# The gate of a hybrid network's second layer, moved into the fill of the feed-forward layer behind it

## Chip, cores, metric

The kernel runs on one core of one Trainium2 chip. A core has five engines, each with an instruction queue of its own that it works through in order: TensorE (PE in the profile; its weight loads are PEld), VectorE (DVE), ScalarE (ACT), GpSimd (POOL) and SyncE (SP), which issues most transfers. Engines wait for each other by semaphores. The metric is the time of one execution in microseconds; lower is better.

## The reference, cut to what matters

Four layers work on an image of 4 x 128 channels x 64 x 64. Only the end of the second and the beginning of the third take part in the change:

```python
# layer 1, its end: o is the state-space branch, turned back to channels
o = (o - mu) * lax.rsqrt(var + 1e-05) * bn_g + bn_b            # over batch and image
g = jax.nn.sigmoid(einsum('bihw,io->bohw', o, conv4_w) + conv4_b)
x = g * x + x
# layer 2: tokens of 128 channels
t = _to_tokens(x)                                              # a transpose
y = _ln_t(t)
attn = products of cos(y + theta) within groups of 8
x1 = layernorm(y + attn)
q = cos(phi) * cos(x1[..., :8])
ffn = relu(q @ w1.T + b1) @ w2.T + b2                          # 8 -> 2048 -> 128
t = t + layernorm(x1 + ffn)
```

The mean and variance of o run over all images, so no gate can be taken before the last map of o is there.

## The kernel before

The whole image stays in on-chip memory as X, 128 partitions x 16384 columns. In the second layer (`layer1`) X holds channels on the partitions; in the third (`layer2`) it holds tokens, 128 x 128 blocks turned in place. All arithmetic is float32.

**End of `layer1`.** The branch's 32 maps of 128 x 512 are stored to device memory as they are made (`kept`, the profile's `o<-o`), with their statistics in `bst` (psy is their psum tile). Behind the last one the statistics are joined (`mv`, line 1404), the normalisation is folded into the weights and bias of the 1x1 convolution (`conv4_w`, `sb`, lines 1404 to 1415), and then 32 gates and 32 turnings are written out, each turning two steps behind its gate:

- `gate(k)`: load map k (`oin`, four buffers, SP's queue, line 1421), a matmul of two passes into `psg`, a sigmoid on ScalarE into `g`, and (g + 1) * X on VectorE back into X;
- `to_tokens(k)`: four 128 x 128 transposes into one psum bank `psf`, and a copy back into X, by VectorE for odd k and by ScalarE for even k.

All but the loads go through `InOrder` (line 82 is its helper, which is why most rows of the profile have line 82): their order on each engine is the order of the program. The loads and what is not wrapped are placed by a scheduler.

**`layer2`.** First its weights: w1T (four loads of 16 KB behind a memset by GpSimd), w2T (1 MB), two zeroed buffers, and the cosine of phi (`cphi`, lines 1503 to 1508). Then 16 groups of 8 token blocks run through a software pipeline. A position p has eight slots; in position p, group p goes through the two big matmuls (`hidden` into `phh`, `rectify` into `hid`, `summed` into `pff`), while group p + 3 gets its first norm (steps a: `moments`, `variance`, `root`, `a_norm`, `a_turns`, `a_less`), group p + 2 its cosines, products and second norm (steps b), and group p - 1 its last norm (steps d). The positions run from -3 to 16. The first three, -3 to -1, have no or hardly any big matmuls: they fill the pipeline. In them the order is: statistics of a (VectorE), root (ScalarE), norm into u (VectorE), u + theta into c (GpSimd), reduction of the angle k, a (VectorE), absolute value and sine (ScalarE), products and u + a (GpSimd), statistics and norm of b (VectorE), gain and bias on x1 (GpSimd), then the angles of q, its sine and its spread into `q8`, which is transposed (`pqt`), copied (`qT`) and fed to `hidden`. The psum pool `ph` has four banks, all under the tag `phh`.

ScalarE evaluates its functions from table sets: the root, the sine and the sigmoid lie in different sets, and a change between them is an instruction of its own, ACT_TABLE_LOAD.

Of the kernel before, what the change touches and what calls it, by code (L numbers as in the profile page):

```python
# [8 lines left out]
F32 = mybir.dt.float32  # L9
I32 = mybir.dt.int32  # L10
AF = mybir.ActivationFunctionType
ALU = mybir.AluOpType
AX = mybir.AxisListType
PSUM = bass.MemoryType.PSUM
DRAM = bass.MemoryType.DRAM

P = 128
NB = 4
# [70 lines left out]
class Kernel:  # L89
# [815 lines left out]

    def layer1(self):

# [4 lines left out]
        tc, X = self.tc, self.X  # L914
        plain = self.nc
        nc = plain
        NG = 8
        GS = NT // NG
        with ExitStack() as ctx:
            cp = ctx.enter_context(tc.tile_pool(name="l1c", bufs=1))  # L920
            sp = ctx.enter_context(tc.tile_pool(name="l1s", bufs=2))
            gp = ctx.enter_context(tc.tile_pool(name="l1g", bufs=2))
            kp = ctx.enter_context(tc.tile_pool(name="l1k", bufs=2))
            dram = ctx.enter_context(tc.tile_pool(name="l1d", bufs=1, space=DRAM))
            pm = ctx.enter_context(tc.tile_pool(name="l1pm", bufs=4, space=PSUM))
            pp = ctx.enter_context(tc.tile_pool(name="l1pp", bufs=1, space=PSUM))

            def mm(name):
                return pm.tile([P, 512], F32, name=name, tag="mm")

            lin1_w = self.load(cp, "lin1_w", [P, P])
            fc_in4 = self.load(cp, "fc_in4", [P, P])
            conv4_w = self.load(cp, "conv4_w", [P, P])


            wx = self.load(cp, "in_w4", [P, 2, 257])
# [8 lines left out]
            ps = mm("psw2")  # L945
# [24 lines left out]

            Y = cp.tile([P, NT + 2 * GS, 2, DI], F32, name="Y")


            CY = [pp.tile([P, 2, 512], F32, name=f"CY{k}") for k in range(2)]
            kept = [dram.tile([P, 512], F32, name=f"o{k}") for k in range(NB * NG)]
            dw = self.col("dw_w")
            sh = [P, GS, 2]

# [83 lines left out]
            def s4(g, dr, j, w=P):  # L1062

                n, i = divmod(g, NG)
                r = GS * i + j
                c = r * P if dr == 0 else (NT - 1 - r) * P + 3
# [333 lines left out]
            nc = plain  # L1400
# [2 lines left out]
            mv = sp.tile([P, 2], F32, name="mv")  # L1403
            nc.vector.bn_aggr(mv, bst)
            sc = sp.tile([P, 1], F32, name="sc")
            sb = sp.tile([P, 1], F32, name="sb")
            nc.scalar.activation(sc, mv[:, 1:2], AF.Sqrt, bias=self.eps5)
            nc.vector.reciprocal(sc, sc)
            nc.vector.tensor_mul(sc, sc, self.col("bn_g"))
# [2 lines left out]
            ps = mm("psg")  # L1412
            nc.tensor.matmul(ps[:, 0:1], conv4_w, sb, start=True, stop=True)
            nc.vector.tensor_add(sb, ps[:, 0:1], self.col("conv4_b"))
            nc.vector.tensor_scalar(conv4_w, conv4_w, sc, None, ALU.mult)
            nc = InOrder(tc)

            def gate(k):
                ks = slice(k * 512, (k + 1) * 512)
                o = gp.tile([P, 512], F32, name="oin", tag="tm", bufs=4)  # L1420
                plain.sync.dma_start(o, kept[k])
                ps = mm("psg")
                nc.tensor.matmul(ps, conv4_w, o, start=True, stop=True)
                g = gp.tile([P, 512], F32, name="g", tag="yT")
                nc.scalar.activation(g, ps, AF.Sigmoid, bias=sb)
                nc.vector.scalar_tensor_tensor(X[:, ks], g, 1.0, X[:, ks], ALU.add, ALU.mult)

            def to_tokens(k):
                ps = mm("psf")
                for v in range(4):  # L1430
                    c = k * 512 + v * P
                    nc.tensor.transpose(ps[:, v * P:(v + 1) * P], X[:, c:c + P], self.ident)
                dst = X[:, k * 512:(k + 1) * 512]
                if k % 2:
                    nc.vector.tensor_copy(dst, ps)
                else:
                    nc.scalar.copy(dst, ps)

            for k in range(NB * NG + 2):
                if k < NB * NG:  # L1440
                    gate(k)
                if k >= 2:
                    to_tokens(k - 2)

    def flip(self):

# [65 lines left out]
    def layer2(self):  # L1512
# [4 lines left out]
        tc = self.tc  # L1517
        nc = self.nc
        GT, NG = 8, NB * NT // 8
        T = self.X.rearrange("p (t c) -> p t c", c=P)  # L1520
        with ExitStack() as ctx:
            cp = ctx.enter_context(tc.tile_pool(name="l2c", bufs=1))
# [4 lines left out]
            ph = ctx.enter_context(tc.tile_pool(name="l2ph", bufs=4, space=PSUM))  # L1527
# [16 lines left out]
            cphi = cp.tile([P, 8], F32, name="cphi")  # L1544
            self.cos(cp, cphi, self.row("phi"), [P, 8], "cphi")

            nc = InOrder(tc)
            V, S, G = nc.vector, nc.scalar, nc.gpsimd

            def bcast(name):  # L1550
# [1 line left out]

            def stream(g):
                return T[:, g * GT:(g + 1) * GT, :]

            st = {}

# [136 lines left out]
            def hidden(g, h, m):  # L1694
                phs = []
                for k in range(NK):
                    ks = slice(32 * k, 32 * k + 32)
                    phh = ph.tile([P, 512], F32, name="phh")
                    nc.tensor.matmul(phh, w1T[ks, m, :], st["qT", g, h][ks, :], start=True, stop=True)
                    phs.append(phh)  # L1700
                return phs

            def rectify(g, h, m, phs, on_vector):
                hids = []
                for k in range(NK):
                    f = NK * m + k
                    hid = hp.tile([P, 512], F32, name="hid")
                    if k in on_vector:
                        V.tensor_scalar(hid, phs[k], b1[:, f:f + 1], 0.0, ALU.add, ALU.max)
                    else:  # L1710
                        S.activation(hid, phs[k], AF.Relu, bias=b1[:, f:f + 1])
                    hids.append(hid)
                st["hid", g, h, m] = hids
# [9 lines left out]
            def on(g, step, *args):  # L1723
                if 0 <= g < NG:
                    step(*([g] + list(args)))

            ON_VECTOR = ((0, 1, 3), (1,), (1,), (1, 3), (1,), (1,), (1, 3), (1,))

            def slot(p, s):
                h, m = divmod(s, 4)  # L1730
                p1, h1, m1 = (p, *divmod(s + 1, 4)) if s < 7 else (p + 1, 0, 0)
                phs = hidden(p1, h1, m1) if 0 <= p1 < NG else None

                if s in (0, 4):
# [12 lines left out]
                if s == 0:  # L1747
                    on(a, lambda g: moments("A", g, stream(g), 0, GT))
                    on(b, lambda g: cosine(st["a", g]))
                    on(b, a_products)  # L1750
                elif s == 1:
                    on(d, d_add, 1)
                    on(a, lambda g: variance("A", g))
                    on(p + 1, lambda g: cosine(st["q", g]))
                    on(p + 1, b_spread)
                elif s == 2:
                    on(d, lambda g: moments("D", g, st["x1", g], 4, GT))
                    on(d, lambda g: variance("D", g))
                    on(b, lambda g: moments("B", g, st["u", g], 0, 4))
                elif s == 3:  # L1760
                    on(b, lambda g: moments("B", g, st["u", g], 4, GT))
                    on(b, lambda g: variance("B", g))
                    for name, g in (("D", d), ("A", a), ("B", b)):
                        on(g, lambda g: root(name, g))
                elif s == 4:
                    on(d, d_ready)
                    on(a, a_norm)
                elif s == 5:
                    on(p, d_add, 0)
                    on(b, b_norm)  # L1770
                    on(d, d_norm, 0)
                elif s == 6:
                    on(d, d_norm, 1)
                    on(d, d_sum)
                    on(a, a_turns)
                    on(p, lambda g: moments("D", g, st["x1", g], 0, 4))
                else:
                    on(a, a_less)
                    on(b, b_turns)

            for p in range(-3, NG + 1):
                for s in range(8):
                    slot(p, s)

# [621 lines left out]
@with_exitstack  # L2406
def tile_conv_attn_hybrid(ctx: ExitStack, tc: tile.TileContext, ins: dict, out: bass.AP):
    k = Kernel(ctx, tc, ins, out)
    k.layer0()
    k.layer1()  # L2410
    k.layer2()
    k.attention_maps(ctx)
    k.moe(2)
    k.attention()
    k.moe(3)
    k.flip()
# [79 lines left out]
```

## Time and profile before

| what | us |
|---|---|
| three runs, median (lowest to highest) | 5611.95 (5593.98 to 5615.91) |
| the profiled execution | 5601.23 |
| its span, first to last instruction | 5599.5 |
| layer 0, to about | 1225 |
| `layer1` up to its joined statistics, to about | 1957 |
| first gate matmul / last token copy | 1957.5 / 2006.2 |
| first statistics of `layer2` | 2004.9 |
| first `phh` matmul / first `pff` matmul | 2057.8 / 2070.0 |
| last `pff` matmuls of `layer2` | 2712 |
| all of the span: busy PE, DVE, ACT, POOL | 4991.9, 4016.3, 3113.9, 3073.1 |

Times inside the execution are counted from the span's start. A row of the profile is a group of instructions: line, engine, operation, tile written <- tiles read, shape. The windows view gives for a stretch how long each engine was busy in it, in microseconds with the number of instructions in brackets, and then the clock that TensorE was granted as a share of full speed, the mean busy share of the sixteen transfer engines, and GB/s. A busy TensorE at half clock does half the work, so both numbers are read together. A VectorE instruction's duration includes time in which it had begun and was held.

### The profile page before, as it was taken

The page shows a single profiled execution, that of the slowest core. Times are in us where ns is not written, and L with a number is a line of the kernel's source. Part 1 is how long each engine was busy: PE and PEld are TensorE (multiplying, and loading weights), DVE is VectorE, ACT ScalarE, POOL GpSimd, SP SyncE. Part 2 cuts the span into 40 slices and gives each one's busy share as a digit, 9 for nine tenths or more (in the row PEclk, how much of TensorE's full clock was granted, in tenths as well). Part 3 has the DMA queues.
Part 4 walks back from the last instruction along what each step waited for, and adds up shares of the span by engine and source line. Part 5 has one row for each costly group of instructions (what it writes and reads, how often), then busy time and mean ns, then how long its engine had stood idle before and what let it go on. Part 6 is the DMA issues. An engine that isn't in the chain of part 4 may idle for free. (4 is left out here: it accounts for less than half of the span.)

```text
span 5599.5 us, 62830 instructions
## 1 busy us (share of the span) xinstructions
PE 4991.9 (89%) x21718; PEld 2404.9 (43%) x21718; DVE 4016.3 (72%) x7854; ACT 3113.9 (56%) x3785; POOL 3073.1 (55%) x3027
## 2 busy tenths in 40 slices
PE   6898989879999859999887899989998998999887
PEld 3454444335656523333443344434433444344443
DVE  6888988758876578786698565666566666665796
ACT  1122222146655345555431689878978987889431
POOL 0525253314444324454399577666766776667597
PEclk8999999989988779999899899999999999999899
DMA  5545454400000020000000000000000000000001
GB/s 171 126 131 128 124 132 127 98 6 1 16 16 12 27 61 1 1 1 1 6 31 16 16 1 1 1 1 1 1 1 1 1 1 1 1 1 1 5 1 61
DMA packets 66743, 185.21 MB, mean 33 GB/s; under 512 B 13158, under 2 KB 16038, under 8 KB 64744
## 3 DMA queue, kind: packets, MB, share of 16 engines
q1 hardware_dynamic: 55792, 163.68, 9.9%
q0 software_dynamic: 6272, 12.86, 1.4%
q10 hardware_dynamic: 4344, 4.50, 0.3%
q8 instruction: 175, 2.87, 0.2%
q14 instruction: 160, 1.31, 0.1%
HBM read 131.63 MB, written 49.36 MB: 32 GB/s over the span
## 5 line engine op out<-in xcount | busy, mean ns | idle before, releaser
L82 POOL TENSOR_TENSOR r<-r 128x512 f32<-128x512 f32 (+1 forms) x1088 | 1349.0, 1241 | 661.9 <-DVE r L82 597.0
L82 DVE TENSOR_TENSOR r<-r,num 128x1024 f32<-128x1024 f32 (+1 forms) x1088 | 970.4, 927 | 564.3 <-PE num L82 514.1
L82 PE MATMUL D<-F,G 32*128 32x512 f32 (+3 forms) x4608 | 1218.8, 589 | 1.9 <-POOL G L82 1.0
L82 PE MATMUL num<-F,G 32*128 32x512 f32 (+3 forms) x4608 | 1084.5, 604 | 105.4 <-DVE r L82 101.6
L82 ACT ACTIVATE r<-r 128x2048 f32<-128x2048 f32 (+4 forms) x610 | 1018.3, 1679 | 49.2 <-POOL r L82 3.4
L82 ACT ACTIVATE r<-D 128x1536 f32<-128x1536 f32 (+1 forms) x544 | 764.2, 1405 | 206.1 <-PE D L82 174.2
L82 PE MATMUL acc<-pr,ident 128*128 128x512 f32 x1600 | 749.4, 619 | 79.4 <-DVE pr L82 79.4
L82 PEld LDWEIGHTS D<-F,G 32*128 32x128 f32 x4608 | 507.2, 189 | 327.4 <-issue 217.2
L82 PE MATMUL acc<-r,v 128*128 128x512 f32 (+3 forms) x1152 | 606.4, 614 | 3.1 <-DVE aT L82 3.1
L82 PEld LDWEIGHTS num<-F,G 32*128 32x128 f32 x4608 | 394.4, 187 | 410.9 <-DVE r L82 239.5
L1886 PE MATMUL pex<-w_expert_w,vT 128*128 128x512 f32 x1024 | 489.5, 618 | 78.9 <-DVE x L1889 78.8
L1896 POOL TENSOR_TENSOR x<-x 128x512 f32<-128x512 f32 (+2 forms) x576 | 472.6, 820 | 103.3 <-DVE x L1889 73.3
L82 PEld LDWEIGHTS acc<-pr,ident 128*128 128x128 f32 x1600 | 309.9, 198 | 439.4 <-issue 340.2
L82 DVE TENSOR_TENSOR pr<-v,wt 128x2560 f32<-128x2560 f32 x160 | 452.7, 2835 | 30.3 <-PE acc L82 24.6
L82 PE MATMUL pff<-hid,w_ffn_w2T 128*128 128x512 f32 x1024 | 468.4, 600 | 0.0
L82 POOL DMA_INDIRECT px<-tab,idx x196 | 330.7, 1687 | 231.5 <-DVE idx L82 159.8
L82 POOL TENSOR_TENSOR X<-X,sl 128x512 f32<-128x512 f32 x32 | 87.9, 2746 | 491.5 <-ACT sl L82 491.5
L1889 DVE TENSOR_TENSOR x<-pex,gate 128x1024 f32<-128x1024 f32 x256 | 309.1, 1213 | 62.8 <-POOL X L1897 51.1
L82 PEld LDWEIGHTS acc<-r,v 128*128 128x128 f32 x1152 | 176.7, 190 | 393.1 <-issue 263.9
L1886 PEld LDWEIGHTS pex<-w_expert_w,vT 128*128 128x128 f32 x1024 | 184.0, 193 | 329.0 <-DVE x L1889 176.9
L82 ACT ACTIVATE hid<-phh,cols 128x512 f32<-128x512 f32 x320 | 198.9, 685 | 224.2 <-PE phh L82 224.2
L82 POOL TENSOR_TENSOR Y<-y,tm 128x64 f32<-128x64 f32 x256 | 115.9, 473 | 331.1 <-DVE w L82 164.3
(563 smaller groups left out, 7379.4 us busy)
## 6 DMA issues: line engine op xcount, KB each, us to landing
v<-tab SPq DMA_DIRECT2D x320, 256.0 KB
oms<-omw SPq DMA_DIRECT2D x32, 432.0 KB
omr<-oms SPq DMA_DIRECT2D x32, 432.0 KB
X<-in_x_dram SPq DMA_DIRECT2D x8, 1024.0 KB
tab<-vb SPq DMA_DIRECT2D x64, 128.0 KB
o<-o SPq DMA_DIRECT2D x32, 256.0 KB
oin<-o SPq DMA_DIRECT2D x32, 256.0 KB
kept<-X SPq DMA_DIRECT2D x4, 2048.0 KB
```

The lines of the kernel that those rows point to most:

```text
L82: return lambda *args, **kwargs: self.tc.keep_in_program_order(op(*args, **kwargs))
L1886: nc.tensor.matmul(pex[:, 4 * h:4 * h + 4, :], vT[:, k, :], ew[:, 512 * h:512 * (h + 1)], start=True, stop=True)
L1889: nc.vector.tensor_tensor(x, pex, gate[:, k, :].unsqueeze(2).to_broadcast([P, NE, P]), ALU.mult)
L1896: nc.gpsimd.tensor_tensor(x[:, 0:w, :], x[:, 0:w, :], x[:, w:2 * w, :], ALU.add)
```

## The change

The gate and the turning to tokens leave `layer1` and become one function `gate(k)` in `layer2`. `layer1` now only prepares `conv4_w`, `sb` and `kept`, in pools that outlive it (`after`, an outer stack in the main function). In `layer2`, 34 steps (32 gates, the turnings two behind) are handed out: four ahead of the first slot, and the rest behind the slots of positions -3, -2 and -1 by the tables GATES (11 steps in a position) and LAST_GATES (8). All copies to tokens are ScalarE's now. The matmul and the transposes use the psum banks of `phh`. The pool of the loaded maps, `l2g`, is opened in `layer2`, behind its weights.

```diff
-    def layer1(self):
+    def layer1(self, after):
...
+        dram = after.enter_context(tc.tile_pool(name="l1d", bufs=1, space=DRAM))
+        ga = after.enter_context(tc.tile_pool(name="l1a", bufs=1))
...
-            conv4_w = self.load(cp, "conv4_w", [P, P])
+            conv4_w = self.load(ga, "conv4_w", [P, P])
...
-            def gate(k):
-                ks = slice(k * 512, (k + 1) * 512)
-                o = gp.tile([P, 512], F32, name="oin", tag="tm", bufs=4)
-                plain.sync.dma_start(o, kept[k])
-                ps = mm("psg")
-                nc.tensor.matmul(ps, conv4_w, o, start=True, stop=True)
-                g = gp.tile([P, 512], F32, name="g", tag="yT")
-                nc.scalar.activation(g, ps, AF.Sigmoid, bias=sb)
-                nc.vector.scalar_tensor_tensor(X[:, ks], g, 1.0, X[:, ks], ALU.add, ALU.mult)
-
-            def to_tokens(k):
-                ps = mm("psf")
-                for v in range(4):
-                    c = k * 512 + v * P
-                    nc.tensor.transpose(ps[:, v * P:(v + 1) * P], X[:, c:c + P], self.ident)
-                dst = X[:, k * 512:(k + 1) * 512]
-                if k % 2:
-                    nc.vector.tensor_copy(dst, ps)
-                else:
-                    nc.scalar.copy(dst, ps)
-
-            for k in range(NB * NG + 2):
-                if k < NB * NG:
-                    gate(k)
-                if k >= 2:
-                    to_tokens(k - 2)
+            self.gate_maps = conv4_w, sb, kept
...
+            conv4_w, gate_b, kept = self.gate_maps
+            gp = ctx.enter_context(tc.tile_pool(name="l2g", bufs=2))
+            NK_ = len(kept)
+
+            def gate(k):
+                if k < NK_:
+                    ks = slice(k * 512, (k + 1) * 512)
+                    o = gp.tile([P, 512], F32, name="oin", bufs=4)
+                    plain.sync.dma_start(o, kept[k])
+                    ps = ph.tile([P, 512], F32, name="psg", tag="phh")
+                    nc.tensor.matmul(ps, conv4_w, o, start=True, stop=True)
+                    x = gp.tile([P, 512], F32, name="g")
+                    S.activation(x, ps, AF.Sigmoid, bias=gate_b)
+                    V.scalar_tensor_tensor(self.X[:, ks], x, 1.0, self.X[:, ks], ALU.add, ALU.mult)
+                if k >= 2:
+                    ps = ph.tile([P, 512], F32, name="psf", tag="phh")
+                    for v in range(4):
+                        c = (k - 2) * 512 + v * P
+                        nc.tensor.transpose(ps[:, v * P:(v + 1) * P], self.X[:, c:c + P], self.ident)
+                    S.copy(self.X[:, (k - 2) * 512:(k - 1) * 512], ps)
...
+            GATES, LAST_GATES = (0, 1, 1, 1, 2, 2, 2, 2), (0, 1, 1, 1, 2, 2, 1, 0)
...
+            steps = iter(range(NK_ + 2))
+            for _ in range(4):
+                gate(next(steps))
             for p in range(-3, NG + 1):
                 for s in range(8):
                     slot(p, s)
+                    for _ in range(GATES[s] if p < -1 else LAST_GATES[s] if p < 0 else 0):
+                        gate(next(steps))
```

In the order that the built program has on SP's queue, the 1 MB load of w2T, the last stores of kept maps and the loads of w1T now stand ahead of the first `oin` load, which waits for the last store to be confirmed; before, the first four `oin` loads stood among the last stores of `layer1`. GpSimd's memsets of w1T and `q8` follow its last work of `layer1`, at the same time as `cphi` on VectorE.

More of the change, by code (lines that the diff above doesn't have):

```diff
@@ L923, in layer1 @@
             kp = ctx.enter_context(tc.tile_pool(name="l1k", bufs=2))
-            dram = ctx.enter_context(tc.tile_pool(name="l1d", bufs=1, space=DRAM))
             pm = ctx.enter_context(tc.tile_pool(name="l1pm", bufs=4, space=PSUM))
@@ L1405, in layer1 @@
             sc = sp.tile([P, 1], F32, name="sc")
-            sb = sp.tile([P, 1], F32, name="sb")
+            sb = ga.tile([P, 1], F32, name="sb")
             nc.scalar.activation(sc, mv[:, 1:2], AF.Sqrt, bias=self.eps5)
@@ L1415, in layer1 @@
             nc.vector.tensor_scalar(conv4_w, conv4_w, sc, None, ALU.mult)
-            nc = InOrder(tc)
-            def gate(k):
-                ks = slice(k * 512, (k + 1) * 512)
-                o = gp.tile([P, 512], F32, name="oin", tag="tm", bufs=4)
-                plain.sync.dma_start(o, kept[k])
-                ps = mm("psg")
-                nc.tensor.matmul(ps, conv4_w, o, start=True, stop=True)
-                g = gp.tile([P, 512], F32, name="g", tag="yT")
-                nc.scalar.activation(g, ps, AF.Sigmoid, bias=sb)
-                nc.vector.scalar_tensor_tensor(X[:, ks], g, 1.0, X[:, ks], ALU.add, ALU.mult)
-            def to_tokens(k):
-                ps = mm("psf")
-                for v in range(4):
-                    c = k * 512 + v * P
-                    nc.tensor.transpose(ps[:, v * P:(v + 1) * P], X[:, c:c + P], self.ident)
-                dst = X[:, k * 512:(k + 1) * 512]
-                if k % 2:
-                    nc.vector.tensor_copy(dst, ps)
-                else:
-                    nc.scalar.copy(dst, ps)
-            for k in range(NB * NG + 2):
-                if k < NB * NG:
-                    gate(k)
-                if k >= 2:
-                    to_tokens(k - 2)
+            self.gate_maps = conv4_w, sb, kept
     def flip(self):
@@ L1545, in layer2 @@
             self.cos(cp, cphi, self.row("phi"), [P, 8], "cphi")
-            nc = InOrder(tc)
+            plain, nc = nc, InOrder(tc)
             V, S, G = nc.vector, nc.scalar, nc.gpsimd
@@ L2409, in tile_conv_attn_hybrid @@
     k.layer0()
-    k.layer1()
-    k.layer2()
+    with ExitStack() as gate:
+        k.layer1(gate)
+        k.layer2()
     k.attention_maps(ctx)
```

## The prediction

> **What bounds the kernel now.** I read the stretches first. This is the windows view: length, then busy time of TensorE, its weight loads, VectorE, ScalarE and GpSimd, the granted clock, the DMA share and GB/s. The cuts are stage borders taken from the timeline: gate stretch to 2004.85, then the feed-forward layer's positions p = -3, -2, -1, then its steady part.
>
> ```profile
> 1957.00:1964.00 7.00, 6.51 (x12) 3.05 (x13) 1.94 (x5) 3.53 (x5) 0.00 (x0) 0.54 0.27 77
> 1964.00:2001.00 37.00, 37.00 (x173) 21.92 (x172) 28.18 (x44) 26.29 (x44) 0.03 (x1) 1.00 0.66 185
> 2004.85:2017.47 12.62, 0.65 (x4) 0.25 (x2) 9.26 (x30) 2.84 (x5) 2.14 (x1) 0.50 0.04 11
> 2017.47:2044.72 27.25, 0.00 (x0) 0.00 (x0) 19.03 (x55) 6.03 (x7) 12.76 (x12) 0.50 0.00 0
> 2044.72:2073.27 28.55, 11.48 (x29) 4.59 (x30) 22.14 (x63) 10.84 (x16) 12.84 (x12) 0.51 0.00 1
> 2073.27:2710.00 636.73, 635.78 (x2268) 252.57 (x2267) 466.57 (x1253) 362.12 (x626) 276.82 (x211) 1.00 0.00 1
> ```
>
> The gate stretch is TensorE without a gap (37.00 of 37.00). The three positions behind it use TensorE hardly at all: they fill a pipeline. From 2073 on TensorE is full to the end of the layer. So the layer ends when its steady part has started plus 637 us, and any time won before 2073 reaches the end undiminished; nothing later touches the gate. Next, the waits of the fill (engine, its instruction, who it waited for, total, times, longest), and then its timeline (start, duration):
>
> ```profile
> PE pqt L82 <- DVE q L82: 43.9, 1, 43.9
> DVE stB L82 <- POOL u L82: 12.7, 2, 7.7
> DVE k L82 <- POOL c L82: 2.3, 1, 2.3
> ```
>
> The fill is one chain through VectorE and GpSimd: VectorE works 9.3 + 19.0 + 22.1 = 50.4 of 68.4 us, and most of its idle time is two waits of 7.7 for GpSimd's products, plus one of 2.3. ScalarE is idle 48.7 of the 68.4.
>
> ```profile
> 1957.49 5.46 PE L82 MATMUL psg<-oin,w_conv_w 128*128 128x512 f32 x6 [0.49 <-PE psg L1413]
> 2000.92 0.34 SPq L118 DMA_DIRECT2D w_ffn_w2T<-in_ffn_w2T_dram  x1
> 2001.53 3.02 SPq L1538 DMA_DIRECT2D w_ffn_w1T<-in_ffn_w1T_dram  x4
> 2018.66 1.28 ACT L82 ACT_TABLE_LOAD   x1
> 2019.95 1.15 ACT L82 ACTIVATE a<-a,halfpi 128x1024 f32<-128x1024 f32 x1
> 2036.83 4.78 POOL L82 TENSOR_TENSOR x<-x,rows 128x1024 f32<-128x1024 f32 x2 [1.97 <-DVE x L82]
> 2037.39 2.37 DVE L82 TENSOR_SCALAR k<-k 128x1024 f32<-128x1024 f32 x1
> 2039.79 2.90 DVE L82 SCALAR_TENSOR_TENSOR a<-k,c 128x1024 f32<-128x1024 f32 x1
> 2042.73 1.22 DVE L82 SCALAR_TENSOR_TENSOR a<-k,a 128x1024 f32<-128x1024 f32 x1
> ```
>
> Two things to see: the same VectorE form takes 2.90 beside a GpSimd multiply and 1.22 without one, and a change of ScalarE's table set costs 1.28.
>
> **The change part by part.** *Removed:* the stretch from the first gate matmul (1957.5) to the fill's first statistics (2004.9), 47.4 us. Its work stays: 32 gates (two matmul passes; sigmoid 0.687 on ScalarE; multiply 0.692 on VectorE) and 32 turnings (four transposes; copy 0.577). The 16 copies that VectorE did (0.684 each, 10.9 us) go to ScalarE (16 x 0.577 = 9.2), which has room. So VectorE gets 32 x 0.692 = 22.1, ScalarE 32 x 1.264 = 40.4, TensorE 32 x 1.30 = 41.5 (its pace in the stretch) at full clock.
>
> *The head.* Before, the first four loads of the kept maps are issued from 1877.2 on, long ahead. Now they stand on SP behind the 1 MB load of w2T, the last store of a kept map and the four w1T loads, and the first waits for that store to land. w2T can be issued once VectorE's mv is done, at 1954.5. Before, it was issued at 2000.9 and its data flowed from about 2003 to 2005.3, at some 410 GB/s; so now until about 1959. The last store (256 KB; such stores ran at 215 to 262 GB/s) follows in the same engines, about 1.1 plus an estimated 1 to be confirmed: 1961. A load issued then, with the same 2 us before data and 0.6 to 1.1 of flow, lets the first gate matmul begin at 1963.5: +6.0. Bounds: +2.5 (first load issued right behind the 3.02 of w1T issues, at about 1957.6, and landing 2.5 later) and +9 (a store confirmed only 3 us later). I take +6, as the order of the queue gives it. GpSimd's memsets also come earlier and hold up VectorE's cphi steps by about 2 us (1.46 and 0.88 instead of 0.17 in the trace of before); that is hidden under these loads, and costs 2 us if they were early.
>
> *Four steps ahead of the fill.* From the first gate matmul to the second token copy took 9.1 (1957.46 to 1966.57), at the clock of 0.54. With that copy now on ScalarE I take 8.5: the fill starts at 1963.5 + 8.5 = 1972.0.
>
> *Position -3* (11 steps): its own 12.6; 11 multiplies of 0.692 on VectorE, +7.6; two of them fall into VectorE's wait for GpSimd's c, but the second is held by it: -1.6. The root needs the square-root set, the next gate the sigmoid set: 1.28 + 0.3 + 1.28 = 2.9, in which ScalarE hands out no gate, and VectorE, in order, has the next multiply ahead of its norm: +2.9. With 0.5 for a slow TensorE step: 22.0. *Position -2* (11 steps): 27.3 + 7.6; one multiply falls into the 7.7 wait, -0.7; roots behind the sigmoid set again, +2.9; the multiplies take over a wait for GpSimd that x bore (first x 2.17 instead of 0.34), -1.8: 35.2. *Position -1* (8 steps, of which 6 still multiply): 28.6 + 4.2 + 2.9 - 0.7 - 1.8 = 33.2. Sum: 1972.0 + 22.0 + 35.2 + 33.2 = 2062.4 against 2073.3, -10.9; I take -10, since each position has another chance of a late gate.
>
> Queued behind a late gate: on TensorE the next gate and turning, then the first qT transposes; on ScalarE the roots and sines; on VectorE the norm. SP holds only further loads of kept maps, each waiting for the matmul four gates ahead; before, four steps were 5.2 us and nobody waited for a load, and now they are longer. ScalarE in position -3 has 11 x 1.264 + 2.9 = 16.8 in 22, in -2 13.9 + 6.0 + 2.6 = 22.5 in 35: covered, though it would become the bound if VectorE's part shrank by 5.
>
> [...] The table: 1.28, and the sine starts 1.29 after the load began. [...] The change adds five returns to the sigmoid set. [...] I take the row. The clock: 0.54 until 1964 although TensorE was busy 93% of it, 1.00 after, 0.50 throughout the fill. [...] At half clock a step costs 1.82 (5.46 / 3) + 1.11 (four transposes) = 2.93 instead of 1.30. My sum keeps full clock for most steps, because in position -3 the demand at half clock, 11 x 2.93 = 32, exceeds the 22 available, so that TensorE would be busy without a break and be granted the full one.
>
> **The time.** The profiled execution took 5601.2 (span 5599.5); the sum makes it 5591. It lies 10.7 under the median of the runs, 5611.95, inside their own spread of 5594 to 5616; I put the difference on the median: 5602.
>
> **The rivals.**
> 1. *The gate hides almost wholly.* If the multiplies fit the waits and TensorE stays at full clock, VectorE only has to do its 50.4 + 19.4 us (28 of the multiplies; four are ahead of the fill) from 1972 on with few gaps: 69.8 + 7 of remaining waits, start of the steady part at 2049, minus 24; with a head of only +2.5 minus 28: 5584 to 5588. For it: 18 us of idle VectorE, 49 of ScalarE. Against: all three engines in order, and the table changes.
> 2. *Slower: TensorE at half clock.* In the front and position -3, 15 steps x 2.93 = 44.0 against 8.5 + 22.0 = 30.5: +13.5. In position -2, 11 x 2.93 = 32.2 is just under 35, but steps come in pairs in one slot and are waited for: +5 over both. -10 + 18.5 = +8.5: 5620. It decides from about six steps at half clock on the path (6 x 1.63 = 10). For it: the clock of 0.50 in all the fill, of 0.54 under 93% load. Against: the self-correction above. [...]
> 3. *No change:* the moved work lengthens the fill by as much as the stretch was, since the chain is in order and the store-then-load head costs 9: about 5610. For it: 6 us of head and 8.7 of table changes are already spent in my sum.
>
> **How the numbers follow.** Likeliest -10: 0.60, its own range 5594 to 5609. Rival 1: 0.16; rival 2: 0.12; rival 3: 0.12. The three runs of before differ by 22 us, 0.4%, so about 0.5% (28 us) is what can be told from no change. Faster by more than that needs under 5584: most of rival 1's edge and a lucky median, 0.14. Slower by more needs over 5640: rival 2 with everything added, 0.05. The rest 0.81. The range takes in rival 1 and rival 2 and the spread of a median: 5578 to 5624.
>
> **What will show it.** First gate matmul near 1963.5, behind w2T and the last store; the fill's stage borders near 1972, 1994, 2029 and 2062; six sigmoid table loads instead of one; gate multiplies of about 2 us beside GpSimd's adds; VectorE waiting for ScalarE's g behind each root; a granted clock well over 0.5 from 1970 to 2030; 637 us of full TensorE behind 2062. Wrong would be: kept-map loads landing later than four steps, the clock at 0.50 in position -3, or the steady part losing its full TensorE.

## The result, and the profile after

The changed kernel takes 5580.66 us, the median of 15 runs (5565.56 to 5591.48); beside it the kernel before took 5601.77 (15 runs, 5590.09 to 5616.25). The ratio is 0.9965, with a 95% interval of 0.9955 to 0.9975: 20 us faster, between 14 and 25. That is less than the 0.5% that I had called distinguishable from three runs, and clear with fifteen.

The profiled execution has a span of 5579.1 us, 20.4 less than the one before. Its windows, cut at the same stage borders as before: from the joined statistics to the first gate matmul (below called the head), to the fill's first statistics (the front), then positions -3, -2, -1, and the steady part to the end of the last `pff` matmul, followed by the same steady part of the kernel before. The columns are again length, TensorE, its weight loads, VectorE, ScalarE, GpSimd, the clock, DMA share, GB/s.

```profile
1944.24:1954.45 10.21, 0.56 (x2) 0.53 (x3) 2.96 (x11) 5.23 (x7) 2.33 (x3) 0.62 0.64 216
1954.45:1962.82 8.37, 8.37 (x21) 4.12 (x22) 2.69 (x5) 3.83 (x7) 0.00 (x0) 0.65 0.51 152
1962.82:1982.29 19.47, 15.40 (x70) 8.26 (x69) 16.75 (x39) 16.71 (x27) 3.08 (x1) 1.00 0.55 162
1982.29:2016.98 34.69, 20.28 (x69) 10.44 (x68) 25.73 (x67) 20.63 (x30) 15.33 (x12) 0.80 0.27 82
2016.98:2050.83 33.85, 21.26 (x71) 11.33 (x70) 25.78 (x69) 21.17 (x32) 14.76 (x12) 0.80 0.06 18
2050.83:2689.42 638.59, 637.41 (x2271) 252.96 (x2270) 466.96 (x1253) 362.08 (x626) 278.90 (x212) 1.00 0.00 1
```

```profile
2073.27:2711.97 638.70, 637.75 (x2272) 253.14 (x2270) 466.57 (x1253) 362.12 (x626) 278.71 (x212) 1.00 0.00 1
```

The steady part took 638.59 us, and 638.70 before: it only starts earlier. The five parts ahead of it sum to 106.6 us from the joined statistics to position 0. Before, that stretch was 119.8 (4.06 to the first gate matmul, 47.36 of gate, 68.42 of fill). So the change itself took 13.3 us out. The other 7 of the two spans' 20 lie ahead of the stretch and behind it: `layer1` from its first `pslin` to its joined statistics took 783.2 us instead of 794.5, what lies ahead of the first `pslin` was 2.1 longer, the later layers about 2. I come back to these.

VectorE's and TensorE's waits of the stretch, from the waits view, and then the head on SP's queue and the first root and its neighbours from the timeline:

```profile
DVE X L82 <- ACT g L82: 21.8, 10, 8.9
DVE stB L82 <- POOL u L82: 8.0, 2, 4.2
PE psg L82 <- DMA oin<-o: 6.5, 1, 6.5
```

```profile
1945.41 0.34 SPq L118 DMA_DIRECT2D w_ffn_w2T<-in_ffn_w2T_dram  x1
1945.84 0.38 SPq L1315 DMA_DIRECT2D o<-o  x1
1946.31 3.04 SPq L1513 DMA_DIRECT2D w_ffn_w1T<-in_ffn_w1T_dram  x4
1951.44 14.25 SPq L1540 DMA_DIRECT2D oin<-o  x11
...
1965.26 1.28 ACT L82 ACT_TABLE_LOAD   x1
1965.34 1.28 DVE L82 SCALAR_TENSOR_TENSOR X<-g,X 128x512 f32<-128x512 f32 x2
1966.56 0.30 ACT L82 ACTIVATE rstdA<-rstdA,eps 128x8 f32<-128x8 f32 x1
1966.87 1.28 ACT L82 ACT_TABLE_LOAD   x1
1968.17 0.69 ACT L82 ACTIVATE g<-psg,sb 128x512 f32<-128x512 f32 x1
1968.89 0.69 DVE L82 SCALAR_TENSOR_TENSOR X<-g,X 128x512 f32<-128x512 f32 x1 [2.26 <-ACT g L82]
1969.73 2.14 DVE L82 TENSOR_SCALAR u<-X,meanA,rstdA 128x128 f32<-128x128 f32 x8
1971.78 1.29 DVE L82 SCALAR_TENSOR_TENSOR X<-g,X 128x512 f32<-128x512 f32 x2
1972.01 3.08 POOL L82 TENSOR_TENSOR c<-u,rows 128x1024 f32<-128x1024 f32 x1 [24.21 <-DVE u L82]
1973.29 2.96 DVE L82 SCALAR_TENSOR_TENSOR X<-g,X 128x512 f32<-128x512 f32 x2 [0.21 <-ACT g L82]
```

Three things to see. The first load of a kept map stands behind w2T, the last store and w1T, and TensorE waits 6.5 us for it. Behind the root, ScalarE loads the sigmoid's set, VectorE waits 2.26 for the gate, and only then norms. And the multiplies at 1973.29 (2.96 for two, where two took 1.29 just before) and GpSimd's c (3.08, before 2.14) hold each other up.

### The profile page after: what moved, and what is told of

It is laid out like the page before. It is cut to its first block, busy times and chain, and to the rows that moved or that the text cites. A ratio compares the mean times of both kernels' runs of the same rounds, so it can differ in the third digit from the quotient of the medians.

```text
span 5579.1 us, 62826 instructions
## 1 busy us (share of the span) xinstructions
PE 4992.0 (89%) x21718; PEld 2403.6 (43%) x21718; DVE 4004.6 (72%) x7838; ACT 3128.2 (56%) x3806; POOL 3079.8 (55%) x3027
## 3 DMA queue, kind: packets, MB, share of 16 engines
q14 instruction: 158, 1.29, 0.1%
## 6 DMA issues: line engine op xcount, KB each, us to landing
X<-in_x_dram SPq DMA_DIRECT2D x8, 1024.0 KB, 10.8
```

## The experiments

I had two groups of questions: what the three costs that the profile shows (head, table load, hold) really weigh on the path, and where the 7 us outside the stretch come from. Each run gave a ratio of whole times, whose interval is 11 to 21 us wide, and one profile, whose stage lengths repeat far better: the stretch from the joined statistics to position 0 was 119.8, 119.7 and 120.3 us in three profiles of kernels with the old gate, and 106.59 and 106.61 in two of the changed one. So parts are judged by the stretch, totals by the ratio.

| kernel | ratio, 95% interval | stretch, us | `layer1`, us |
|---|---|---|---|
| before (profile shown first) | 1 | 119.8 | 794.5 |
| changed | 0.9965, 0.9955 to 0.9975 | 106.6 | 783.2 |
| pools moved alone | 0.9991, 0.9973 to 1.0009 | 119.7 | 797.3 |
| before, again | 0.9994, 0.9980 to 1.0008 | 120.3 | 797.0 |
| changed, again | 0.9965, 0.9948 to 0.9982 | 106.6 | 783.3 |
| all 34 steps in front | 0.9994, 0.9978 to 1.0010 | 121.0 | 792.2 |
| head: loads in `layer1` | 0.9963, 0.9951 to 0.9976 | 102.8 | 787.0 |
| no sigmoid | 0.9962, 0.9949 to 0.9974 | 101.5 | 786.4 |
| gate in psum | 0.9972, 0.9961 to 0.9984 | 101.6 | 777.9 |
| half of the copies on VectorE | 0.9990, 0.9979 to 1.0001 | 110.2 | 783.6 |
| step behind the norm | 0.9960, 0.9946 to 0.9974 | 100.7 | 805.6 |
| warm front | 0.9948, 0.9929 to 0.9966 | 103.2 | 786.3 |
| three edits | 0.9957, 0.9938 to 0.9976 | 92.4 | 790.3 |
| three edits, warm | 0.9948, 0.9928 to 0.9968 | 91.7 | 780.9 |

### 1. Pools moved, gate where it was

```diff
+        dram = after.enter_context(tc.tile_pool(name="l1d", bufs=1, space=DRAM))
+        ga = after.enter_context(tc.tile_pool(name="l1a", bufs=1))
...
-            conv4_w = self.load(cp, "conv4_w", [P, P])
+            conv4_w = self.load(ga, "conv4_w", [P, P])
```

> The kernel before, with only the two pools moved out of layer1 (the maps' device memory, conv4_w and its bias); the gate stays where it was. In the two profiles layer1, from its first pslin to its joined statistics, took 794.5 us before and 783.2 after. Theory pools (the new places of the tiles shorten layer1): some 9 us faster than before, layer1 at 783 to 787. Theory loads (the four early loads of kept maps, which the change takes out of layer1's tail, held its stores): no difference to before, 0 +- 4 us, layer1 at 794. Theory chance (the clock granted in layer1 differs from one execution to the next): no difference in the medians, layer1 anywhere from 783 to 795.

`layer1` took 797.3 us, and the ratio is 0.9991 with 1 inside its interval. The moved pools don't shorten anything.

### 2. All steps ahead of the first slot

```diff
-            for _ in range(4):
+            for _ in range(NK_ + 2):
                 gate(next(steps))
...
-                    for _ in range(GATES[s] if p < -1 else LAST_GATES[s] if p < 0 else 0):
-                        gate(next(steps))
```

> The changed kernel with all 34 steps ahead of the first slot, so nothing stands between the slots. My sum: head +6, the gate stretch 47.4 as before, the fill 68.4 as before, so 123 to 127 us from the joined statistics to position 0, against 119.8 before and 106.6 after. Theory chance: in all 4 to 8 us slower than before. Theories pools and loads (layer1 is shorter by 9 in every kernel with the change's layer1): 1 to 5 us faster than before. In both, 17 to 21 us slower than the changed kernel.

The stretch was 121.0: head 10.3, gate 43.3, fill 67.4. My sum was 123 to 127; the gate ran 4 us faster than in `layer1` (all its copies are on ScalarE, and the clock was 0.96 instead of 0.93; which of the two did it, no run separates). So the move alone costs 1 us (head +6.2, gate -4.0, fill -1.0), and the interleaving is what brought 14.4: 121.0 against 106.6.

This kernel's `layer1` has on TensorE, VectorE, ScalarE, GpSimd and SP the same instructions in the same order as the changed one, and takes its tiles from the same pools; it took 792.2 us against 783.2. So the theory that the change's `layer1` is shorter in every kernel is not borne out.

### 3. The head: first loads issued in `layer1`

The buffers of `tm`, free at the end of `layer1`, are moved to a pool that outlives it and receive the first loads.

```diff
+            first = []
+            for k in range(4):
+                o = ga.tile([P, 512], F32, name="oin", tag="tm", bufs=4)
+                plain.sync.dma_start(o, kept[k])
+                first.append(o)
...
-                    o = gp.tile([P, 512], F32, name="oin", bufs=4)
-                    plain.sync.dma_start(o, kept[k])
+                    if k < 4:
+                        o = first[k]
+                    else:
+                        o = ga.tile([P, 512], F32, name="oin", tag="tm", bufs=4)
+                        plain.sync.dma_start(o, kept[k])
```

> The changed kernel with the first four loads of kept maps issued at the end of layer1, ahead of the load of w2T (their buffers outlive layer1). My head step: the first gate matmul comes 4 us behind the joined statistics as before, not 10.2, so 6 us faster than the changed kernel, some 26 faster than before. Rival (the loads of the maps 4 to 7, still behind w2T and w1T, become the wait instead): 2 to 3 us faster than the changed kernel. Theory loads: layer1 is back at 794, which eats it up: 3 us slower than the changed kernel.

The first gate matmul came 4.3 us behind the joined statistics instead of 10.2, the 5.9 that the head step gave, and the later loads were in time. But the stretch fell only by 3.8. The rest was given back in position -1, 35.8 instead of 33.9, by something that I had not thought of. Its timeline on VectorE:

```profile
2029.65 0.20 DVE L82 RECIPROCAL rstdB<-rstdB 128x8 f32<-128x8 f32 x1
2031.00 0.11 DVE L1950 MEMSET has<- 128x64 f32 x1 [1.16 <-ACT g L82]
2031.03 2.67 DVE L82 TENSOR_SCALAR x<-u,meanB,rstdB 128x128 f32<-128x128 f32 x8
...
2037.42 1.83 DVE L1959 COPY last<-ident 128x128 f32<-128x128 f32 x1
```

Lines 1946 to 1978 prepare the attention of a later layer. Some 5 us of VectorE's time for such lines lie in position -1 of this run; in the fill of the changed kernel there are none. I take it that their tiles now fell on the buffers that the gate had just set free, so that the scheduler could place them here, in the middle of the fill, where VectorE is in demand. That is my reading; what speaks for it is that these lines are gone again in the run with three edits, where those buffers are lent out.

### 4. No sigmoid

Identity in its place; the sigmoid is left out.

```diff
-                    S.activation(x, ps, AF.Sigmoid, bias=gate_b)
+                    S.activation(x, ps, AF.Identity, bias=gate_b)
```

> The changed kernel with Identity in place of the sigmoid, which leaves the sigmoid out; everything else stays. It needs no table set of its own, so the changes between the root and the next gate fall away. My step (2.9 us in each of three positions, all on the path): 8 to 9 us faster than the changed kernel, and VectorE's three waits of 2.3 behind the roots shrink below 0.7. Rival (the table changes are hidden beside other waits of the fill): 0 to 3 us faster.

The stretch fell by 5.1, to 101.5: 1.4, 1.4 and 2.3 in the three positions and nothing ahead of them. Between my 8 to 9 and the rival's 0 to 3. VectorE's waits for g in the three positions (total, times, longest; first of the changed kernel, then of this run) fell:

```profile
DVE X L82 <- ACT g L82: 10.8, 7, 2.4
DVE X L82 <- ACT g L82: 4.1, 6, 0.9
```

But its two waits for GpSimd's u grew from 8.0 to 9.2: a part of what it won it had to wait for later. The rows of the first root show the rest:

```profile
1968.65 1.28 ACT L82 ACT_TABLE_LOAD   x1
1968.73 1.28 DVE L82 SCALAR_TENSOR_TENSOR X<-g,X 128x512 f32<-128x512 f32 x2
1969.95 0.30 ACT L82 ACTIVATE rstdA<-rstdA,eps 128x8 f32<-128x8 f32 x1
1970.15 0.67 ACT L82 ACTIVATE g<-psg,sb 128x512 f32<-128x512 f32 x1
1970.85 0.69 DVE L82 SCALAR_TENSOR_TENSOR X<-g,X 128x512 f32<-128x512 f32 x1 [0.84 <-ACT g L82]
```

The load of the root's set is still there, and lies beside two multiplies of VectorE, here as in the changed kernel. Only the load back to the sigmoid's set had been on the path. (In positions -2 and -1 two such returns fall away, one behind a sine and one behind a root; the load of the root's set lies there in VectorE's wait for GpSimd's u, 4.2 us in position -2.)

### 5. The gate kept in psum

```diff
-                    x = gp.tile([P, 512], F32, name="g")
+                    x = ps
                     S.activation(x, ps, AF.Sigmoid, bias=gate_b)
```

> The changed kernel with the sigmoid written back into its psum bank, so that VectorE's gate multiply reads psum and X and no longer two tiles of on-chip memory. Theory hold (VectorE and GpSimd keep each other from that memory: multiplies of 2.36 instead of 0.69, GpSimd's c of 3.08 instead of 2.14): the multiplies beside GpSimd's work stay under 0.9, c is back at 2.14 to 2.2, and the joined statistics to position 0 takes 3 to 5 us less than 106.6. Rival (the form does not matter, the holds stay): 0 +- 1. Second rival (each gate holds its psum bank until its multiply is done, and the four banks run out): 2 to 6 us longer, with TensorE waiting for VectorE's X.

The stretch fell by 5.0, to 101.6. In the first position GpSimd and VectorE now read:

```profile
1960.40 1.88 DVE L82 SCALAR_TENSOR_TENSOR X<-psg,X 128x512 f32<-128x512 f32 x3
1960.62 2.16 POOL L82 TENSOR_TENSOR c<-u,rows 128x1024 f32<-128x1024 f32 x1 [24.20 <-DVE u L82]
```

Three multiplies in 1.88 beside a c of 2.16; c was 2.16, 2.15 and 2.16 in the three positions, where it had been 3.08, 3.15 and 3.14. Theory hold stands. The rows of the changed kernel agree: its c ended at 1975.09, 2.02 behind the end of the two multiplies that were running when it began (1973.07), and the two held multiplies ended 1.16 behind c. The four psum banks did not run out: VectorE waited for the gate as long as before (10.8 us), and TensorE's waits for VectorE's X fell from 17.0 to 10.5.

### 6. Half of the copies back on VectorE

```diff
-                    S.copy(self.X[:, (k - 2) * 512:(k - 1) * 512], ps)
+                    dst = self.X[:, (k - 2) * 512:(k - 1) * 512]
+                    if k % 2:
+                        V.tensor_copy(dst, ps)
+                    else:
+                        S.copy(dst, ps)
```

> The changed kernel with every second copy to tokens back on VectorE, as before the change; 15 of them fall into positions -3 to -1. My step (VectorE's own work sets the fill, 0.684 a copy): 8 to 11 us longer from the joined statistics to position 0, so 115 to 118, and in all some 10 us slower than the changed kernel. Rival (they fit the waits of VectorE, 10.8 us for g and 8.0 for GpSimd's u in the profile after): 0 to 3 us longer.

The stretch grew by 3.6, to 110.2: 2.9 of it in the three positions, for 15 copies of 0.68. That is near the rival's 0 to 3 and far from my 8 to 11. VectorE's waits for g fell from 10.8 to 6.4 us and those for u from 8.0 to 6.4, and ScalarE had 15 copies less. So work added to VectorE in the fill costs about 0.2 us for 0.68, net of what ScalarE saves. The ratio, 0.9990, is 14 us above the changed kernel's, more than the stretch explains; the two intervals are so wide that 2 and 26 would fit too.

### 7. The step between root and norm put behind the norm

```diff
-            GATES, LAST_GATES = (0, 1, 1, 1, 2, 2, 2, 2), (0, 1, 1, 1, 2, 2, 1, 0)
+            GATES, LAST_GATES = (0, 1, 1, 0, 3, 2, 2, 2), (0, 1, 1, 0, 3, 2, 1, 0)
```

> The changed kernel with the one step that stands between a root and its norm put behind the norm (slots 3 and 4 hold 0 and 3 steps instead of 1 and 2). Theory table (VectorE's waits of 2.26, 2.3 and 2.37 behind the roots are the load of the sigmoid's set and the gate behind it, and nothing else needs that time): each of the three falls by about 2, the joined statistics to position 0 takes 4 to 6 us less than 106.6. Rival (the wait only moves behind the norm, where the next multiply waits for its g, or GpSimd's c is held by one more multiply): 0 to 2 us less.

The stretch fell by 5.9, to 100.7; 4.6 of this in the positions (0.7, 1.9, 2.0), the rest in the front, which the edit does not touch and which was granted a clock of 0.79 instead of 0.65. The first root:

```profile
1984.82 0.30 ACT L82 ACTIVATE rstdA<-rstdA,eps 128x8 f32<-128x8 f32 x1
1985.14 1.28 ACT L82 ACT_TABLE_LOAD   x1
1985.15 0.20 DVE L82 RECIPROCAL rstdA<-rstdA 128x8 f32<-128x8 f32 x1 [0.26 <-ACT rstdA L82]
1985.39 2.14 DVE L82 TENSOR_SCALAR u<-X,meanA,rstdA 128x128 f32<-128x128 f32 x8
1986.43 0.69 ACT L82 ACTIVATE g<-psg,sb 128x512 f32<-128x512 f32 x1
1987.44 3.86 DVE L82 SCALAR_TENSOR_TENSOR X<-g,X 128x512 f32<-128x512 f32 x3
```

The table load now lies beside the norm, VectorE waits 0.26 for the root where it had waited 2.26 for the gate, and the gate is ready before VectorE is. Over the three positions its waits for g fell from 10.8 to 5.2. Theory table stands: almost all that leaving out the sigmoid brought can be had with the sigmoid. Not all of the 4.6 need be the table, though: GpSimd's c was held less too, 2.48, 2.70 and 2.69 instead of 3.08, 3.15 and 3.14, which is 1.5 us in all.

### 8. Before, again; changed, again

> The kernel before, unchanged, once more. Theory chance (layer1's 794.5 against 783.2 in the two profiles is the clock that this execution was granted): ratio 1 within 0.002; layer1 anywhere from 783 to 797, so away from 794.5 by several us is likely. Theory that the change shortens layer1: layer1 at 792 to 797 again, as in the two profiles of kernels with the gate in layer1 (794.5, 797.3).

> The changed kernel once more, unchanged. Theory chance (of its 20 us, 13 belong to the stretch between joined statistics and position 0; the rest is the clock granted in layer1 in that profile): 105.5 to 107.5 us in the stretch again, ratio 0.9965 to 0.9990, layer1 anywhere from 778 to 806. Theory that the change shortens other parts too: ratio 0.9950 to 0.9970 and layer1 near 783 again.

The kernel before gave 0.9994 of itself, and `layer1` at 797.0; the changed one 0.9965 again, a stretch of 106.61, and `layer1` at 783.3. Here neither theory wins outright. That `layer1` came out 0.1 us from its first value speaks against chance. But the run of the step behind the norm, whose `layer1` has the same instructions in the same order too, took 805.6 us in it, more than any kernel before. Its window, and that of the gate in psum, from the first `pslin` to the joined statistics:

```profile
1158.26:1963.85 805.59, 732.51 (x3665) 462.39 (x3664) 562.67 (x1686) 428.08 (x787) 301.69 (x527) 0.86 0.03 11
```

```profile
1155.00:1932.86 777.86, 702.90 (x3665) 441.60 (x3664) 560.02 (x1685) 428.06 (x786) 302.32 (x527) 0.90 0.03 11
```

The same 3665 matmuls, VectorE and ScalarE busy to within 3 us; what differs is the clock, 0.86 against 0.90, and with it 30 us of TensorE. In all fourteen profiles the length of this stage less TensorE's busy time in it lies between 70 and 76 us. A spread of 28 us in one stage whose instructions don't change is more than the whole effect that was to be measured.

The better test is over all runs. For each kernel I take 5600 us times (ratio - 1), and subtract the change of its stretch: what is left is time outside of it. For the changed kernel that is -19.6 + 13.2 = -6.4 us, both times. For the two kernels that have the old gate (pools moved, before again) it is -4.8 and -3.8, though nothing was changed there. For the nine others it is -4.5, -3.7, -2.9, +2.5, +4.0, -3.2, -12.4, +3.3 and -1.0, in the order of the table: a mean of -2.0. So no saving outside of the stretch stands out from what an unchanged kernel shows. That the six microseconds are nothing is not shown either; the intervals are 6 us to each side at best.

### 9. A warm front

20 transposes of the identity that nobody reads, in TensorE's wait for the first load.

```diff
+            for _ in range(5):
+                ps = ph.tile([P, 512], F32, name="psw", tag="phh")
+                for v in range(4):
+                    nc.tensor.transpose(ps[:, v * P:(v + 1) * P], self.ident, self.ident)
             steps = iter(range(NK_ + 2))
```

> The changed kernel with 20 idle transposes of the identity on TensorE ahead of the first gate, in the wait for its load. They compute nothing that is used. Theory clock (the first steps of the gate ran at a granted clock of 0.65, and that is on the path): granted near 1.00 from the first gate matmul on, front 6 to 7 us instead of 8.4, position -3 as it was, 1.5 to 2.5 us less from the joined statistics to position 0. Rival (the clock does not rise in 5 us of transposes, or the four steps wait for ScalarE and VectorE and not for TensorE): 0 +- 0.7 us. Second rival (the transposes end behind the landing of the first map): up to 2 us more.

The front took 5.74 us instead of 8.37, at a granted clock of 1.00 instead of 0.65; the stretch fell by 3.4, of which 2.6 in the front and 0.9 in position -1. The ratio, 0.9948, would be 29 us, some 12 more than the stretch explains, with an interval of 10 us to each side. TensorE's timeline, first of this run and then of the changed kernel:

```profile
1948.00 4.50 PE L82 MATMUL psw<-ident 128*128 128x128 f32 x20 [0.34 <-DVE sb L1416]
1954.29 3.07 PE L82 MATMUL psg<-oin,w_conv_w 128*128 128x512 f32 x6 [1.79 <-DMA oin<-o]
1957.20 0.60 PE L82 MATMUL psf<-ident,X 128*128 128x128 f32 x4
```

```profile
1954.45 5.46 PE L82 MATMUL psg<-oin,w_conv_w 128*128 128x512 f32 x6 [6.51 <-DMA oin<-o]
1959.70 0.88 PE L82 MATMUL psf<-ident,X 128*128 128x128 f32 x4
```

The first three gates took 3.07 instead of 5.46, behind the 1.79 us in which TensorE had stood.

The 0.9 us of position -1 come from one more gate. At the end of position -2 the changed kernel ran one at half clock (granted 0.51), and ScalarE waited for it ahead of the absolute value and the sine; here that gate ran at full clock. First the changed kernel, then this run:

```profile
2013.03 1.91 PE L82 MATMUL psg<-oin,w_conv_w 128*128 128x512 f32 x2
2014.98 0.69 ACT L82 ACTIVATE g<-psg,sb 128x512 f32<-128x512 f32 x1 [1.12 <-PE psg L82]
```

```profile
2011.13 1.02 PE L82 MATMUL psg<-oin,w_conv_w 128*128 128x512 f32 x2
2012.31 1.06 ACT L82 ACTIVATE a<-a 128x1024 f32<-128x1024 f32 x1 [0.25 <-DVE a L82]
```

The absolute value began 1.88 us ahead of position -1, and 0.95 in the changed kernel. In this run an earlier gate ran at half clock instead (1.92 us at 2005.83), where the next sigmoid waited for VectorE anyway. So the 0.9 shows what one such gate can cost, not that the warm-up keeps the clock full that late.

### 10. Three edits together, and warm

The head's loads in `layer1`, the gate in psum, and the step behind the norm. The buffers of the head are lent to `ff` for the rest of the layer, so that the tiles of the later layer find no room there:

```diff
-                st["ff", g, h] = hp.tile([P, 512], F32, name="ff", bufs=2)
+                st["ff", g, h] = ga.tile([P, 512], F32, name="ff", tag="tm", bufs=4)
```

> The changed kernel with three edits together: the first four loads of kept maps issued at the end of layer1 (and their buffers then lent to ff, so that nothing of a later layer finds room to start early), the sigmoid written back into its psum bank, and slots 3 and 4 with 0 and 3 steps. Alone, they took 5.9 (the head), 5.0 and 4.6 us (positions only) from the 106.6 us between the joined statistics and position 0. If the three lie on one chain, one behind the other, they add up: 91 us, some 28 us faster than before, ratio 0.9945 to 0.996. Rival (a second chain, ScalarE's 1.26 a step and its table loads or GpSimd's products, becomes the bound): 94 to 98 us, ratio 0.9955 to 0.997.

92.4 us against 91.1 by addition, and under the rival's 94 to 98: for the most part the three costs lie one behind the other on one chain. By parts it is less exact. The head gave its 5.9. The three positions gave 7.5, where the gate in psum and the moved step alone had given 5.0 and 4.6; both shorten c, so they overlap. The front gave 0.7 that none of the edits was meant to give, at a clock of 0.71 instead of 0.65. On VectorE no line of a later layer is left in the fill. The last version adds 12 transposes of the identity at the end of `layer1`:

> The three edits of the run with all together, and 12 idle transposes of the identity on TensorE between the last psy matmul of layer1 and the bias of the gate, where TensorE waits some 4 us; they compute nothing that is used. Theory clock (the first gates run at half clock and are on the path): front 5 to 6 us instead of 7.6, so 89.5 to 91 us from the joined statistics to position 0 instead of 92.4; some 29 us faster than before, ratio 0.9940 to 0.9960. Rival (3.3 us of transposes are too few for the clock, or they push the bias back): 92 to 93.5 us.

The stretch was 91.7, between my 89.5 to 91 and the rival's 92 to 93.5: the front took 7.14 instead of 7.64. The timeline shows why:

```profile
1937.26 1.47 PE L82 MATMUL psw<-ident 128*128 128x128 f32 x12
1941.27 0.35 PE L1419 MATMUL psg<-sb,w_conv_w 128*128 128x1 f32 x2 [2.53 <-issue]
1942.27 4.28 PE L82 MATMUL psg<-oin,w_conv_w 128*128 128x512 f32 x6 [0.65 <-DVE w_conv_w L1421]
```

The transposes took 1.47 us and not 3.3, and TensorE then stood for 2.5 us. The granted clock was 1.00 from 1938.20 to 1942.27, and 0.76 in the front behind it; the first three gates took 4.28, where the warm front had 3.07. A warm-up counted in instructions missed. All the same this is the fastest kernel of the study by stretch: 5566.63 us, 0.9948 of before (0.9928 to 0.9968). Beside it the changed kernel took 5581.20. The 14.6 us between them agree with the 14.9 between the two stretches, though the intervals of the two ratios overlap.

## Why the prediction was right, and where not

The sign and the size class were right, and the chain of the fill was the right place to look. Step by step:

- **The level.** 5602 was the profile's 5601.2 less 10 plus 10.7, because the median of three runs lay above the profile. Over fifteen runs before has a median of 5601.77, so those 10 us were chance of three runs. This step failed: the sum should have stood on the profile, at 5591. It is half of the 21 us between forecast and measured time.
- **The bound.** Time won before position 0 reaches the layer's end: the steady part took 638.70 us before and 638.59 after (637.6 to 640.9 in the other runs). Right.
- **Head +6.0:** +6.15, with the queue as described, and 5.9 taken back by moving the loads. Right. The 1 us in it for the store's confirmation was an estimate that no run shows alone: in the changed kernel the transfers ran at 228 GB/s in the half microsecond up to 1951.0 and at 18 in the one behind it, and the first load was issued at 1951.44.
- **Four steps 8.5:** 8.4. Right as a sum, and I had taken the half clock for given; warm it is 5.7.
- **Position -3, 22.0:** 19.5. **Position -2, 35.2:** 34.7. **Position -1, 33.2:** 33.9. Together 88.0 instead of 90.4. The mis-sized term is the table change, 2.9 in each position, both loads with the root between them: it measured 1.4, 1.4 and 2.3. The load of the root's set begins while VectorE still multiplies or waits for GpSimd, and only the return is on the path. That makes the sum 3.6 too long, of which 1.2 is offset elsewhere.
- **VectorE's work at its full price.** The sum counted each multiply at 0.69 but for the few that I put into waits. Added copies of 0.68 cost 0.2 net, so VectorE's waits absorb most of such work; that the same holds for the multiplies was not measured. On the other side, the sum had no term for c being held (3.08 instead of 2.14), and the holds together measured 5.0 by the gate in psum. These are two errors of opposite sign, so that the positions came out within 2.4 us is in part luck.
- **A row misread.** `DVE stB <- POOL u: 12.7, 2, 7.7` gives the total, the number and the longest of the waits: the two were 7.7 and 5.1, not 7.7 each. The sum took 0.7 out of each, so it does not change.
- **The row for the table change.** It held: 1.28, and the sigmoid starts 1.30 behind the start of the load (1966.87 to 1968.17).
- **The clock.** 0.65 in the front, 1.00 in position -3, 0.80 in the two behind it. Full clock for most steps, as the sum had it. The reason given for it was not the real one: in position -3 TensorE was not busy without a break but 15.4 of 19.5 us, and kept 1.00; why, no run shows. Nor does one show the slow step for which the sum had put 0.5 into that position. *Rival 2* fell with it: of the fifteen steps that it put at half clock in the front and position -3, the eleven of position -3 ran at full clock, and the front cost 2.6 us, where the rival had taken 1.63 a step. But some gates in the last two positions did run at half clock (1.91 to 2.08 us for two passes instead of 1.02). One of them cost 0.9; what the others cost was not measured.
- **Rival 1**, the gate hidden almost wholly, put the whole change at -24 to -28. The changed kernel is at -13.3, short of it by what head, table and hold cost; with these three mended the stretch is at -27.4 (and its head at nothing, which the rival had not assumed). So the cover was there, as the rival said, but not open to the order as it was written.
- **Rival 3** fell: the positions grew by 19.6 us and the head with its front by 14.5, together 34 for the 47 removed.
- **The sum.** -10.9 for the stretch, -13.3 measured. The whole time fell by 20 (14 to 25); the difference of 6 has no place that the runs could show. The 5580.66 lies under the 5594 to 5609 of the case that I held likeliest, and even under the 5584 to 5588 of rival 1; it is within the 5578 to 5624 by 3 us. That room had been left for rival 1, which did not come true, so here too luck had a part.

## What to carry to other kernels

When work is slotted into a chain that runs in order, its price is set less by its own microseconds than by what it stands between: here one step between a root and its norm, in each of three positions, cost 4.6 us in all, more than fifteen copies put on VectorE (2.9), and moving that step by one slot got it back. Read three things for each inserted piece: what it waits for where it stands (2.26 us behind the first root), which neighbour reads the same memory at that moment (c 3.08 instead of 2.14), and which queue its loads have to pass (a wait of 6.5 us). And judge a local change by its own stretch of the profile, which repeated here within 0.6 us while `layer1` ahead of it moved by 28; but don't move the level of a forecast by a median of three.

## What was not expected of the hardware

- TensorE's clock moved one stage of 3665 unchanged matmuls between 778 and 806 us (granted 0.90 and 0.86).
- 20 transposes of the identity, busy 4.50 us in all, were enough for a granted 1.00 behind a pause of 1.79 us; 12 of them in 1.47 us, followed by pauses of 2.5 and 0.65 us, were not (granted 0.76).
- The hold between VectorE and GpSimd went away with one operand in psum: GpSimd's c back from 3.08 to 2.16, the multiplies beside it from 1.48 to 0.63 each.
